# The end of the attention rows: x1 of the last two pairs turned back by TensorE, the last pair row by row, and a shorter chain for its group norm

## The chip, the core and the metric

The kernel runs on one core of a Trainium2 chip. The metric is the device time of one execution in microseconds (us); the time before is the median of three runs. The core has five engines that work side by side, each through its own instruction stream in order: PE (TensorE, matrix products; its weight loads are shown apart as PEld), DVE (VectorE), ACT (ScalarE), POOL (GpSimd) and SP (SyncE, which here only issues DMA transfers). Engines wait for each other through semaphores. PE and DVE/ACT exchange data through PSUM, everything else lies in SBUF or, for large arrays, in DRAM.

## What is computed

The input `x` has 256 rows of 256 positions with 128 channels. Two layers are added to it in turn. The first is a group norm followed by attention along each row, with gates:

```python
# layer 0
q = norm(x) @ wq.T / sqrt(32);  k = kv_x @ wk.T;  v = kv_x @ wv.T        # 4 heads of 32
a = softmax(q @ k.T + bias1 + bias2)
o = (a @ v) * sigmoid(norm(x) @ wg.T + bg)
x1 = x + (o @ wo.T + bo)
# layer 1
y = x1 + fourier_layer(group_norm(x1))
# group_norm: over all positions and the 4 channels of a group
m = mean(v, axis=(1, 2, 4)); s = var(v, axis=(1, 2, 4))
out = (v - m) / sqrt(s + 1e-5)
```

The Fourier layer of layer 1 begins with a transform along the positions of a row and one across the rows. The first of these is linear and needs no norm, so it is taken in layer 0 already, row by row, out of `x1`; the norm is brought in later through a scaled matrix.

## The kernel before

All arithmetic is float32. `layer0` first takes the statistics of `x`, then runs `Rows.run`, a loop over the 256 rows, which are handled in pairs (128 pairs, `g`) where that is possible. For each row `s` of a pair the loop issues, on a schedule written out by hand (within it, instructions stand on each engine in the order of the source):

- `scores(s)`: PE multiplies q and k of the four heads into two PSUM tiles `sc`, one for two heads; ACT takes the exponential. That of the first two heads stays in PSUM, that of the other two goes to SBUF (`e[1]`).
- `weigh(s)`: the factor exp(bias1) is multiplied in, by DVE for the first two heads (L354), by POOL for the other two (L359). POOL also adds the two halves of each (`es`, L364), as half of the softmax sums.
- `attend(s)`: PE multiplies by v (L374) and by ones (L379, the sums); DVE forms the gated quotient in three steps on 128x256 (L385, L386 reciprocal, L387) and leaves it in `gate`.
- `out(g)`, two steps of the loop after the second row's scores: PE multiplies both rows' `gate` by `wo`, DVE adds bias and x in place (L394), so that `turned` holds x1 with the channels on the partitions; DVE turns it in blocks of 32 (L396) and SP stores it to `x1d` in DRAM in four DMAs (L400), for layer 1.
- `again(g)` (L405) loads the same pair back from `x1d`, now with the positions on the partitions; `squares(g)` (L410, ACT) sums the squares per row into `Q2`; `spectrum(g)`, later, multiplies by the transform matrix `adft` on PE into `u` and ACT copies it to `U` (L420).

So x1 goes to DRAM and back between `out` and `spectrum`, and the loop runs five steps beyond the last row to finish the last pairs. In the last of these, `spectrum` runs for pairs 126 and 127. After each 32 rows `row_sums` (L193, L194) reduces U's first column and Q2 into `mv2`.

After the loop, `Groups.load` loads the averaging matrix `gavg` and a raw transform matrix (L81, L82) on SP, into space that the row loop's constants held. `Groups.make` computes mean and rstd of each channel group: it sums `mv2` (L89), scales, forms the variance per channel, averages over the group with two products by `gavg` (L50, L57 in `group_stats`, each brought back by an ACT copy), takes the root and one Newton step (`rsqrt`, L35 to L43), and scales the transform matrix into `bdft` (L94). Beside it runs a flag (L170 to L181): whether the biases were so large that the rows must be done over in a slower, safe form (`layer0_general`); its root on ACT (L176) makes the flag NaN in the bad case. All engines read the flag and branch (L183). Here the branch skips the slow form. The first matmul of layer 1 is `dps` (L964): it multiplies U by `bdft`. Layer 1's loads of constants (L605 onwards) and of weights (L803, L827) follow on SP; what a scheduler puts ahead of the branch and what behind it isn't written by hand.

Of the kernel before, what the change touches and what calls it, by code (L numbers as in the profile page):

```python
# [10 lines left out]
FP = mybir.dt.float32  # L11
AF = mybir.ActivationFunctionType
ALU = mybir.AluOpType
# [32 lines left out]
def group_stats(nc, pool, psum, mv, gavg, tag):  # L46

    mr = pool.tile([P, 2], FP, tag=tag + "_mr", name=tag + "_mr")
    ps = psum.tile([P, 512], FP, tag="a", name=tag + "_ps")
    nc.tensor.matmul(ps[:, 0:1], gavg, mv[:, 0:1], start=True, stop=True)  # L50
    nc.scalar.copy(mr[:, 0:1], ps[:, 0:1])
    d = pool.tile([P, 1], FP, tag=tag + "_d", name=tag + "_d")
    nc.vector.tensor_sub(d, mv[:, 0:1], mr[:, 0:1])
    nc.vector.tensor_mul(d, d, d)
    nc.vector.tensor_add(d, d, mv[:, 1:2])
    ps2 = psum.tile([P, 512], FP, tag="a", name=tag + "_ps2")
    nc.tensor.matmul(ps2[:, 0:1], gavg, d, start=True, stop=True)  # L57
# [12 lines left out]
class Groups:  # L70
# [13 lines left out]
    def make(self, pool, psum, mv2, tag):  # L84

        nc = self.nc
        mv = pool.tile([P, 2], FP, name=tag + "mv")
        m2 = pool.tile([P, 1], FP, name=tag + "m2")
        nc.vector.tensor_reduce(mv, mv2.rearrange("p k s -> p s k"), AX.X, ALU.add)  # L89
        nc.vector.tensor_scalar(mv, mv, 1.0 / 65536, None, ALU.mult)  # L90
        nc.vector.tensor_mul(m2, mv[:, 0:1], mv[:, 0:1])
        nc.vector.tensor_sub(mv[:, 1:2], mv[:, 1:2], m2)
        nc.vector.tensor_copy(self.mr, group_stats(nc, pool, psum, mv, self.gavg, tag))
        nc.vector.tensor_scalar(self.bdft, self.raw, self.mr[:, 1:2], None, ALU.mult)  # L94


def layer0(tc, I, C, ident, x1d, U, Q2, mv2, groups):
# [92 lines left out]
def row_sums(nc, U, Q2, mv2, k):  # L190

    t = slice(32 * k, 32 * k + 32)
    nc.vector.tensor_reduce(mv2[:, k, 0:1], U[:, 0, t], AX.X, ALU.add)  # L193
    nc.vector.tensor_reduce(mv2[:, k, 1:2], Q2[:, t], AX.X, ALU.add)  # L194


class Rows:
# [72 lines left out]
    def run(self):  # L270
# [16 lines left out]
        def row(s):  # L287
            return pairs[s // 2], slice(256 * (s % 2), 256 * (s % 2) + 256)
# [36 lines left out]
        def scores(s):  # L325

            r = rows[s]
            qkT = r["qkT"]
            sc = [ps_s.tile([P, 2, 512], FP, tag=f"s{hp}", name=f"sc_{s}_{hp}") for hp in range(2)]
            for c in range(2):  # L330
                for h in range(4):
                    p = slice(32 * h, 32 * h + 32)
                    nc.tensor.matmul(  # L333
                        sc[h // 2][:, h % 2, c * 256 : (c + 1) * 256],
                        qkT[p, 256 + c * P : 256 + (c + 1) * P], qkT[p, 0:256],
                        start=True, stop=True,
                    )
# [11 lines left out]
            r["sc"] = sc[0]  # L349

        def weigh(s):

            r = rows[s]
            nc.vector.tensor_tensor(  # L354
                r["e"][0].rearrange("p h c q -> p (h c q)"), r.pop("sc").rearrange("p h x -> p (h x)"),
                b1T[:, 0:2].rearrange("p h c q -> p (h c q)"), ALU.mult,
            )
            e1 = r["e"][1].rearrange("p h c q -> p (h c q)")
            nc.gpsimd.tensor_tensor(e1, e1, b1T[:, 2:4].rearrange("p h c q -> p (h c q)"), ALU.mult)  # L359
# [29 lines left out]
        def out(g):  # L389
            p = pairs[g]  # L390
            ps = ps_a.tile([P, 512], FP, tag="a", name=f"wo_{g}")
            by_columns(ps, wT["wo"], p.pop("gate"))
            xT = p["xT"]
            nc.vector.scalar_tensor_tensor(xT, ps, self.bo, xT, ALU.add, ALU.add)  # L394
            t = wk.tile([P, 16, 32], FP, tag="xb", name=f"x1b_{g}", bufs=1)
            nc.vector.transpose(t.rearrange("p b c -> p (b c)"), xT)  # L396
            pieces = self.x1d[2 * g : 2 * g + 2].rearrange("s (b t) c -> t (s b) c", t=32)
            for a in range(4):
                ch = slice(32 * a, 32 * a + 32)
                nc.sync.dma_start(pieces[:, :, ch], t[ch])  # L400

        def again(g):
            p = pairs[g]
            p["x1"] = wk.tile([P, 2, 2, P], FP, tag="x1", name=f"x1_{g}")
            nc.sync.dma_start(p["x1"], self.x1d[2 * g : 2 * g + 2].rearrange("s (j p) c -> p s j c", p=P))  # L405

        def squares(g):
            for s in (2 * g, 2 * g + 1):
                p, q = row(s)
                nc.scalar.activation(p["xT"][:, q], p["xT"][:, q], AF.Square, accum_out=self.Q2[:, s : s + 1])  # L410

        def spectrum(g):
            x1 = pairs.pop(g)["x1"]
# [6 lines left out]
            nc.scalar.copy(  # L420
                self.U[:, :, 2 * g : 2 * g + 2], ps[:, 0:258].rearrange("p (s f) -> p f s", s=2)
            )
# [3 lines left out]

        with tc.manual_schedule(engines={ENG.PE, ENG.Activation, ENG.DVE, ENG.Pool, ENG.SP}):
            turn(0)
            for i in range(-1, NS + 5):
                g, odd = i // 2, i % 2  # L430
                if odd and whole(g - 2):
                    again(g - 2)
                    squares(g - 2)
                if not odd and whole(g):
                    gates(g)
                if 0 <= i < NS:
                    scores(i)
                if i + 1 < NS:
                    project(i + 1)
                if 0 <= i < NS:  # L440
                    exp = rows[i].pop("exp")
                    exp(1, 0)
                    exp(1, 1)
                    weigh(i)
                if odd and whole(g + 1):
                    values(g + 1)
                if odd and whole(g + 2):
                    turn(g + 2)
                if not odd and whole(g - 2):
                    out(g - 2)  # L450
                if not odd and whole(g - 4):
                    spectrum(g - 4)
                if i == NS + 4:
                    spectrum(g - 3)
                if 8 <= i < 16:
                    k, h = divmod(i - 8, 4)
                    nc.vector.tensor_reduce(
                        bad[:, k, h : h + 1], b1T[:, h].rearrange("p c q -> p (c q)"), AX.X,
                        ALU.min if k else ALU.max,
                    )  # L460
                if i == 16:
                    hi, lo = bad[:, 0, 7:8], bad[:, 1, 7:8]
                    nc.vector.tensor_reduce(hi, bad[:, 0, 0:4], AX.X, ALU.max)
                    nc.vector.tensor_reduce(lo, bad[:, 1, 0:4], AX.X, ALU.min)
                    nc.vector.tensor_scalar(hi, hi, math.exp(BIAS_MAX) * E_SCALE, None, ALU.is_le)
                    nc.vector.tensor_scalar(lo, lo, math.exp(BIAS_MIN) * E_SCALE, None, ALU.is_ge)
                    nc.vector.tensor_mul(hi, hi, lo)
                if i % 32 == 11 and i > 32:
                    row_sums(nc, self.U, self.Q2, self.mv2, i // 32 - 1)
                if 0 <= i - 1 < NS:  # L470
                    attend(i - 1)
            row_sums(nc, self.U, self.Q2, self.mv2, 7)


# [1659 lines left out]
```

## Time and profile before

| | us |
|---|---|
| median of three runs | 2658.32 (2653.32 to 2668.18) |
| the profiled execution, by the clock of the runs | 2673.89 |
| its span, first to last instruction | 2672.1 |
| input statistics of layer 0, to the first row | 0 to 155 |
| row loop in its steady state | 155 to 1427 |
| end of the rows, group norm, branch | 1427 to 1459 |
| layer 1 | 1459 to 2672 |

Over the whole span PE is busy for 2426.5 us (91%), DVE for 2027.5 (76%), POOL for 1488.8 (56%) and ACT for 1421.3 (53%). The mean clock granted to PE is 0.941 of full speed. A busy share is an average over stages that have different limits, so it is read by stage.

In the lines that follow, an entry such as `DVE L387` names the engine and the line of the kernel; `out<-in` are the names of what is written and read, followed by sizes (partitions x elements) and the number of instructions merged (x8). In a timeline the first number is the start in us from the beginning of the span, the second the duration; in square brackets stands the idle time of the engine just before, and who ended it. Times of a tile's DMA are of its issue on SP; landing comes later.

### The profile page before, as it was taken

To read this page: it belongs to the slowest core of one execution; us is meant where nothing else is said; L and a number is where in the kernel's file an instruction comes from. 1 tells how busy PE (TensorE), PEld (TensorE's weight loads), DVE (VectorE), ACT (ScalarE), POOL (GpSimd) and SP (SyncE) were. 2 spreads that over 40 slices of the span, in tenths; PEclk is the share of its full clock that TensorE was granted. 3 is DMA by queue.
4 is the path that set the end of the run, shared out by engine and by line. 5 is a ranking of instruction groups with operands and counts; after the bars stand their busy time and mean duration, and the time that the engine had idled before them with its cause. 6 is when DMAs were issued, how large, how long until landed. Compare 5 with 4: busy or idle time off the path is not lost. (4 is left out here: it accounts for less than half of the span.)

```text
span 2672.1 us, 88760 instructions
## 1 busy us (share of the span) xinstructions
PE 2426.5 (91%) x37572; PEld 1549.0 (58%) x37572; DVE 2027.5 (76%) x2886; ACT 1421.3 (53%) x2718; POOL 1488.8 (56%) x1042
## 2 busy tenths in 40 slices
PE   6699999999999999999997999998979978898754
PEld 6555655555656555565554567786755456444533
DVE  6799999999999999999996457566546654465455
ACT  0278888888888888888884122001016401555232
POOL 1199999999999999999994012002136411111211
PEclk8899999999999999999998989999989988899855
DMA  9755666556566666565652011888877764997598
GB/s 348 222 91 100 107 105 107 101 104 105 105 105 109 107 107 108 102 106 103 109 101 63 4 58 47 274 272 289 297 264 265 239 223 149 332 359 260 192 386 344
DMA packets 1017925, 459.02 MB, mean 172 GB/s; under 512 B 831094, under 2 KB 947273, under 8 KB 1011128
## 3 DMA queue, kind: packets, MB, share of 16 engines
q1 hardware_dynamic: 977720, 363.13, 54.1%
q0 software_dynamic: 22912, 81.80, 7.9%
q10 hardware_dynamic: 16896, 8.39, 1.1%
q8 instruction: 298, 4.88, 0.8%
q14 instruction: 99, 0.81, 0.1%
HBM read 317.89 MB, written 135.27 MB: 170 GB/s over the span
## 5 line engine op out<-in xcount | busy, mean ns | idle before, releaser
L359 POOL TENSOR_TENSOR e<-e,b1T 128x1024 f32<-128x1024 f32 x256 | 607.1, 2372 | 143.8 <-DMA xk<-in_x_dram 76.2
L364 POOL TENSOR_TENSOR es<-e 128x512 f32<-128x512 f32 x512 | 648.4, 1289 | 0.0
L386 DVE RECIPROCAL av<-av 128x256 f32<-128x256 f32 x256 | 452.1, 1766 | 9.1
L342 ACT ACTIVATE sc<-sc,b2T 128x512 f32<-128x512 f32 x512 | 338.7, 662 | 122.9 <-PE sc L333 110.8
L342 ACT ACTIVATE e<-sc,b2T 128x512 f32<-128x512 f32 x512 | 324.7, 694 | 0.0
L354 DVE TENSOR_TENSOR e<-sc,b1T 128x1024 f32<-128x1024 f32 x256 | 310.9, 1215 | 9.7 <-ACT sc L342 9.3
L333 PE MATMUL sc<-qkT 32*128 32x256 f32 x4096 | 293.9, 400 | 3.4 <-DVE e L354 3.4
L1392 PE MATMUL yps<-xt,mpT 128*128 128x256 f32 x1024 | 252.8, 398 | 29.2 <-DVE yt L1404 12.6
L374 PE MATMUL av<-e,v 128*32 128x256 f32 x4096 | 269.1, 379 | 1.8 <-DVE gate L387 1.7
L333 PEld LDWEIGHTS sc<-qkT 32*128 32x128 f32 x4096 | 185.5, 184 | 115.2 <-issue 53.0
L1392 PEld LDWEIGHTS yps<-xt,mpT 128*128 128x128 f32 x1024 | 195.7, 197 | 75.4 <-DVE yt L1404 18.7
L374 PEld LDWEIGHTS av<-e,v 128*32 128x32 f32 x4096 | 130.0, 109 | 126.1 <-issue 38.3
L1408 POOL DMA_DIRECT2D yd<-yt x32 | 17.5, 546 | 320.2 <-DVE yt L1404 317.5
L308 ACT ACTIVATE qkT<-qk,qb 128x512 f32<-128x512 f32 x256 | 174.4, 681 | 7.5 <-PE qk L285 7.5
L285 PEld LDWEIGHTS u<-adft,x 128*32 128x32 f32 x4096 | 120.6, 111 | 82.7 <-issue 78.6
L285 PE MATMUL qk<-turned,wn_wq 128*32 128x256 f32 x2048 | 164.5, 393 | 1.8 <-DVE turned L293 1.8
L410 ACT ACTIVATE turned<-turned 128x256 f32<-128x256 f32 x256 | 104.4, 408 | 113.7 <-DVE x1b L396 111.4
L379 PE MATMUL av<-es,ones 128*32 128x256 f32 x2048 | 161.1, 379 | 1.6 <-POOL es L364 1.6
L285 PE MATMUL qk<-turned,wT_wk 128*32 128x256 f32 x2048 | 158.4, 381 | 0.0
L293 DVE STREAM_TRANSPOSE turned<-xk 128x1024 f32<-128x1024 f32 x128 | 157.9, 1234 | 0.1
L1795 ACT ACTIVATE blocks<-h2ps,col 128x512 f32<-128x512 f32 x128 | 88.9, 777 | 128.3 <-PE h2ps L1259 128.3
L285 PE MATMUL u<-adft,x 128*32 128x129 f32 x4096 | 139.5, 276 | 6.2 <-DMA x<-x1d 6.2
(532 smaller groups left out, 4177.7 us busy)
## 6 DMA issues: line engine op xcount, KB each, us to landing
xt<-x1d SPq DMA_DIRECT2D x128, 512.0 KB, 7.8
xb<-in_x_dram SPq DMA_DIRECT2D x32, 1024.0 KB, 7.8
xk<-in_x_dram SPq DMA_DIRECT2D x512, 64.0 KB, 3.1
xk<-in_L_conv_kv_x_dram SPq DMA_DIRECT2D x512, 64.0 KB, 2.5
x1d<-x1b SPq DMA_DIRECT2D x512, 64.0 KB, 2.2
x<-x1d SPq DMA_DIRECT2D x128, 256.0 KB, 3.2
y<-yd SPq DMA_DIRECT2D x62, 512.0 KB, 6.3
gs<-Gd SPq DMA_DIRECT2D x384, 64.0 KB, 5.3
```

What stands on the lines that cost most here:

```text
L285: nc.tensor.matmul(out[hd], w[:, hd], src, start=start, stop=stop)
L293: nc.vector.transpose(turned[:, a : b + 1 : b - a].rearrange("p k (b c) -> p k b c", c=32), t)
L308: nc.scalar.activation(r["qkT"], ps, AF.Identity, bias=self.qb)
L333: nc.tensor.matmul(sc[h // 2][:, h % 2, c * 256 : (c + 1) * 256], qkT[p, 256 + c * P : 256 + (c + 1) * P], qkT[p, 0:256], start=True, stop ...
L342: nc.scalar.activation(r["e"][1][:, :, c, :] if hp else z, z, AF.Exp, bias=b2T[:, c, s : s + 1])
L354: nc.vector.tensor_tensor(r["e"][0].rearrange("p h c q -> p (h c q)"), r.pop("sc").rearrange("p h x -> p (h x)"), b1T[:, 0:2].rearrange("p ...
L359: nc.gpsimd.tensor_tensor(e1, e1, b1T[:, 2:4].rearrange("p h c q -> p (h c q)"), ALU.mult)
L364: nc.gpsimd.tensor_tensor(es, e[:, :, 0, :], e[:, :, 1, :], ALU.add)
L374: nc.tensor.matmul(ps[hd, 0:256], p["v"][:, 2 * (s % 2) + c, hd], r["e"][h // 2][:, h % 2, c, :], start=(c == 0), stop=(c == 1),)
L379: nc.tensor.matmul(ps[32 * h : 32 * h + 32, 256:512], self.ones, r["es"][h // 2][:, h % 2, :], start=True, stop=True,)
L386: nc.vector.reciprocal(rd, rd)
L1392: nc.tensor.matmul(rows_of(ps[j]), mpT[:, sc, tt], by_turn(xt[:, sc])[:, j], start=(sc == 0), stop=False,)
```

## The change

Five edits belong together. Row 255 (the last) has the exponential of its second pair of heads kept in PSUM and weighed by DVE in place of POOL. The output projection of the last pair is done row by row (`out_row`), row 254 ahead of the attention product of row 255, into the PSUM tiles of the scores, which are free by then. Pairs 126 and 127 are no longer read back from DRAM: PE transposes `turned` with the identity, ACT copies the result into the tile that the load would have filled (`back`). The loop ends after row 255's attention; what is left stands behind it in a row. And `Groups.make` sums first and second moments over the group in one product of two columns and forms the variance of the group directly, without the step over the channels' own variances.

```diff
     def make(self, pool, psum, mv2, tag):
...
+        n = 1.0 / 65536
         mv = pool.tile([P, 2], FP, name=tag + "mv")
...
         nc.vector.tensor_reduce(mv, mv2.rearrange("p k s -> p s k"), AX.X, ALU.add)
-        nc.vector.tensor_scalar(mv, mv, 1.0 / 65536, None, ALU.mult)
-        nc.vector.tensor_mul(m2, mv[:, 0:1], mv[:, 0:1])
-        nc.vector.tensor_sub(mv[:, 1:2], mv[:, 1:2], m2)
-        nc.vector.tensor_copy(self.mr, group_stats(nc, pool, psum, mv, self.gavg, tag))
-        nc.vector.tensor_scalar(self.bdft, self.raw, self.mr[:, 1:2], None, ALU.mult)
+        ps = psum.tile([P, 512], FP, tag="a", name=tag + "_ps")
+        nc.tensor.matmul(ps[:, 0:2], self.gavg, mv, start=True, stop=True)
+        nc.vector.tensor_scalar(minus, ps[:, 0:1], -n, None, ALU.mult)
+        nc.vector.tensor_scalar(sq, ps[:, 1:2], n, EPS, ALU.mult, ALU.add)
+        nc.vector.tensor_scalar(mean, ps[:, 0:1], n, None, ALU.mult)
+        nc.vector.scalar_tensor_tensor(ve, mean, minus, sq, ALU.mult, ALU.add)
+        nc.scalar.activation(r, ve, AF.Sqrt)
+        nc.vector.reciprocal(r, r)
+        nc.vector.scalar_tensor_tensor(sq, r, r, ve, ALU.mult, ALU.mult)
+        nc.vector.tensor_scalar(sq, sq, -0.5, 1.5, ALU.mult, ALU.add)
+        nc.vector.tensor_mul(rstd, r, sq)
+        nc.vector.tensor_scalar(self.bdft, self.raw, rstd, None, ALU.mult)
...
                 nc.scalar.activation(
-                    r["e"][1][:, :, c, :] if hp else z, z, AF.Exp, bias=b2T[:, c, s : s + 1]
+                    r["e"][1][:, :, c, :] if hp and s < NS - 1 else z, z, AF.Exp, bias=b2T[:, c, s : s + 1]
                 )
...
         def weigh(s):
...
+            for hp, sc in enumerate(r.pop("sc")):
+                e = r["e"][hp].rearrange("p h c q -> p (h c q)")
+                w = b1T[:, 2 * hp : 2 * hp + 2].rearrange("p h c q -> p (h c q)")
+                if hp == 0 or s == NS - 1:
+                    nc.vector.tensor_tensor(e, sc.rearrange("p h x -> p (h x)"), w, ALU.mult)
+                else:
+                    nc.gpsimd.tensor_tensor(e, e, w, ALU.mult)
...
+        def back(g, ps, rows=(0, 1)):
+            p = pairs[g]
+            if "x1" not in p:
+                p["x1"] = wk.tile([P, 2, 2, P], FP, tag="x1", name=f"x1_{g}")
+            for s in rows:
+                for k in (2 * s, 2 * s + 1):
+                    nc.tensor.transpose(ps[:, k * P : (k + 1) * P], p["xT"][:, k * P : (k + 1) * P], self.ident)
+                nc.scalar.copy(
+                    p["x1"][:, s].rearrange("p j c -> p (j c)"), ps[:, 2 * s * P : (2 * s + 2) * P]
+                )
+
+        def out_row(s, ps):
+            p, q = row(s)
+            by_columns(ps[:, q], wT["wo"], p["gate"][:, q])
+            xT = p["xT"][:, q]
+            nc.vector.scalar_tensor_tensor(xT, ps[:, q], self.bo, xT, ALU.add, ALU.add)
...
-            for i in range(-1, NS + 5):
+            for i in range(-1, NS + 1):
...
-                if i == NS + 4:
-                    spectrum(g - 3)
...
+                if i == NS:
+                    last = [ps_s.tile([P, 2, 512], FP, tag=f"s{k}", name=f"last_{k}")[:, 0] for k in range(2)]
+                    out_row(NS - 2, last[0])
                 if 0 <= i - 1 < NS:
                     attend(i - 1)
+            g = NS // 2 - 1
+            back(g - 1, ps_a.tile([P, 512], FP, tag="a", name=f"back_{g - 1}"))
+            spectrum(g - 2)
+            squares(g - 1)
+            spectrum(g - 1)
+            back(g, last[1], (0,))
+            out_row(NS - 1, last[0])
+            store(g)
+            back(g, last[1], (1,))
+            squares(g)
+            spectrum(g)
             row_sums(nc, self.U, self.Q2, self.mv2, 7)
```

`store(g)` is the second half of the old `out(g)` (L396, L400) as a function of its own, `squares(g)` is what it was. As built, four weight loads of layer 1 (`pwr_w`, `mxr_w`, `w24r`, `w24i`), which stood on SP ahead of the branch, stand behind layer 1's `psw` loads; on all engines the order of everything else outside this stretch is the same.

More of the change, by code (lines that the diff above doesn't have):

```diff
@@ L86, in make @@
         nc = self.nc
+        n = 1.0 / 65536
         mv = pool.tile([P, 2], FP, name=tag + "mv")
-        m2 = pool.tile([P, 1], FP, name=tag + "m2")
+        t = pool.tile([P, 4], FP, name=tag + "t")
+        minus, sq, ve, r = (t[:, k : k + 1] for k in range(4))
+        mean, rstd = self.mr[:, 0:1], self.mr[:, 1:2]
         nc.vector.tensor_reduce(mv, mv2.rearrange("p k s -> p s k"), AX.X, ALU.add)
-        nc.vector.tensor_scalar(mv, mv, 1.0 / 65536, None, ALU.mult)
-        nc.vector.tensor_mul(m2, mv[:, 0:1], mv[:, 0:1])
-        nc.vector.tensor_sub(mv[:, 1:2], mv[:, 1:2], m2)
-        nc.vector.tensor_copy(self.mr, group_stats(nc, pool, psum, mv, self.gavg, tag))
-        nc.vector.tensor_scalar(self.bdft, self.raw, self.mr[:, 1:2], None, ALU.mult)
+        ps = psum.tile([P, 512], FP, tag="a", name=tag + "_ps")
[10 more added lines that the diff above has]
+        nc.vector.tensor_scalar(self.bdft, self.raw, rstd, None, ALU.mult)
 def layer0(tc, I, C, ident, x1d, U, Q2, mv2, groups):
@@ L348, in scores @@
             r["exp"] = exp
-            r["sc"] = sc[0]
+            r["sc"] = sc
         def weigh(s):
             r = rows[s]
[L354 to L359, printed above, removed]
+            for hp, sc in enumerate(r.pop("sc")):
[5 more added lines that the diff above has]
+                    nc.gpsimd.tensor_tensor(e, e, w, ALU.mult)
             r["es"] = []
@@ L394, in out, with store @@
             nc.vector.scalar_tensor_tensor(xT, ps, self.bo, xT, ALU.add, ALU.add)
+            store(g)
+        def store(g):
             t = wk.tile([P, 16, 32], FP, tag="xb", name=f"x1b_{g}", bufs=1)
-            nc.vector.transpose(t.rearrange("p b c -> p (b c)"), xT)
+            nc.vector.transpose(t.rearrange("p b c -> p (b c)"), pairs[g]["xT"])
             pieces = self.x1d[2 * g : 2 * g + 2].rearrange("s (b t) c -> t (s b) c", t=32)
@@ L405, in again, with square @@
             nc.sync.dma_start(p["x1"], self.x1d[2 * g : 2 * g + 2].rearrange("s (j p) c -> p s j c", p=P))
+        def square(s):
+            p, q = row(s)
+            nc.scalar.activation(p["xT"][:, q], p["xT"][:, q], AF.Square, accum_out=self.Q2[:, s : s + 1])
         def squares(g):
-            for s in (2 * g, 2 * g + 1):
-                p, q = row(s)
-                nc.scalar.activation(p["xT"][:, q], p["xT"][:, q], AF.Square, accum_out=self.Q2[:, s : s + 1])
+            square(2 * g)
+            square(2 * g + 1)
         def spectrum(g):
-            x1 = pairs.pop(g)["x1"]
+            x1 = pairs[g]["x1"]
             ps = ps_a.tile([P, 512], FP, tag="a", name=f"u_{g}")
@@ L469, in run @@
                     row_sums(nc, self.U, self.Q2, self.mv2, i // 32 - 1)
+                if i == NS:
+                    last = [ps_s.tile([P, 2, 512], FP, tag=f"s{k}", name=f"last_{k}")[:, 0] for k in range(2)]
+                    out_row(NS - 2, last[0])
                 if 0 <= i - 1 < NS:
                     attend(i - 1)
+            g = NS // 2 - 1
[5 more added lines that the diff above has]
+            out_row(NS - 1, last[0])
+            store(g)
+            back(g, last[1], (1,))
+            squares(g)
+            spectrum(g)
             row_sums(nc, self.U, self.Q2, self.mv2, 7)
```

## The prediction, made before the changed kernel ran

> **What bounds the kernel now.** I read the page first, then the timeline of the stretch the diff touches, the waits of that stretch and a table by stage. From the page:
>
> ```profile
> span 2672.1 us, 88760 instructions
> ```
>
> The profiled execution took 2673.89 us by the clock of the runs, 1.8 us more than its span and 15.6 us above the median of 2658.32. All sums below are made against this execution; the difference they give is then taken off the median.
>
> The edit sits between the last scores of the row loop (about 1427 us) and the first matmul of layer 1 (1459.10 us). By stage (columns: length, then busy time of PE, weight loads, DVE, ACT, POOL, then granted clock, DMA share, GB/s):
>
> ```profile
> 155.00:1427.00 1272.00, 1269.47 (x23818) 758.96 (x23820) 1233.75 (x1392) 1045.03 (x2109) 1206.07 (x745) 1.00 0.59 104
> 1427.00:1459.00 32.00, 16.24 (x214) 9.45 (x206) 14.73 (x37) 8.50 (x25) 8.54 (x6) 0.74 0.28 58
> ```
>
> Two things to see. In the row loop PE is never idle, so nothing there is worth editing; in the 32 us behind it no engine is busy half the time and PE's clock falls to 0.74. This is a chain of latencies, and nothing of layer 1 can run beside it, since layer 1's first matmul needs `bdft`, its last product. What is cut from this chain should come off the whole time. The chain in the timeline (start, duration, in brackets the idle time before and who ended it):
>
> ```profile
> 1438.52 0.42 DVE L387 SCALAR_TENSOR_TENSOR gate<-av,gate 128x256 f32<-128x256 f32 x1
> 1439.09 1.94 PE L285 MATMUL wo<-gate,wT_wo 128*32 128x512 f32 x8 [2.87 <-DVE gate L387]
> 1441.08 0.75 DVE L394 SCALAR_TENSOR_TENSOR turned<-wo,bo,turned 128x512 f32<-128x512 f32 x1 [2.14 <-PE wo L285]
> 1441.92 0.36 SPq L81 DMA_DIRECT2D gavg<-const_gavg_dram  x1
> 1443.22 0.37 SPq L405 DMA_DIRECT2D x<-x1d  x1
> 1443.70 2.15 SPq L400 DMA_DIRECT2D x1d<-x1b  x4
> 1446.18 1.95 PE L285 MATMUL u<-adft,x 128*32 128x129 f32 x32 [3.65 <-DMA x<-x1d]
> 1447.75 0.40 SPq L405 DMA_DIRECT2D x<-x1d  x1
> 1450.66 1.95 PE L285 MATMUL u<-adft,x 128*32 128x129 f32 x32 [2.53 <-DMA x<-x1d]
> 1453.07 0.19 DVE L193 TENSOR_REDUCE mv<-U 128x1 f32<-128x32 f32 x1 [10.49 <-ACT U L420]
> 1454.80 1.28 ACT L176 ACT_TABLE_LOAD   x1
> 1456.57 0.20 ACT L37 ACTIVATE g_r<-g_ve 128x1 f32<-128x1 f32 x1 [0.22 <-DVE g_ve L35]
> 1457.98 0.29 DVE L94 TENSOR_SCALAR bdft<-bdft,mr 128x128 f32<-128x128 f32 x1
> 1459.10 3.67 PE L964 MATMUL dps<-U,bdft 128*64 128x512 f32 x8 [3.03 <-DVEq L183]
> ```
>
> Pair 126 was finished at 1435.6, yet its reload is issued only at 1443.22: in SP's queue it stands behind `gavg`, which waits until the last L394 has read `bo`. Pair 127 goes to DRAM and back: L394 ends at 1441.83, its spectrum starts at 1450.66. DVE stands idle for 10.49 us.
>
> [...]the stores took 2.2 us from issue to landing, the reload issued at 1443.22 released PE at 1446.18. A round trip is two of these. [...]after 2.87 us of idling the `wo` matmuls took 1.94 us where the loop's take 1.04, and `u` 1.95 instead of 1.07.[...]
>
> **The change, part by part.**
>
> *e1 of row 255 from POOL to DVE.* Before, POOL multiplied it from 1430.71 to 1433.08 and its two sums ended at 1435.6, which released av(255) and so L385 at 1436.26. Now DVE multiplies it straight behind e0 (ends 1430.61) in 1.21 us, to 1431.85; the exponentials write PSUM and end near 1430.5 either way. POOL's sums can end at 1433.3, 2.3 us sooner. But the queue behind e1 on DVE pays: attend(254) starts at 1431.88 instead of 1431.47, so gate(254) is ready at 1434.55 (was 1434.14).
>
> *Row 254's output projection ahead of av(255).* PE runs in order, so av(255), which waited for POOL, now waits behind `last` for gate(254): 1434.70 with the 0.15 us latency seen at 1438.94 to 1439.09. `last` is eight passes of 256 columns, pitch 0.45 us as for `qk`; av(255) follows from 1435.15, its ones-part from 1436.0 to 1436.65. L385 can start at 1436.67, 0.4 us later than before. So what POOL gave, PE's order takes back, and I book +0.4 us. Had it come out fully it would have been worth about 2 us. Row 254's 256-wide add on DVE (0.42 us, as L385) fits in the gap ahead of L385. gate(255) is then ready at 1436.67 + 2.68 (the old span of L385 to L387) = 1439.35.
>
> *Turning back by TensorE.* PE now has work in that window: four transposes for pair 126 in two steps (the second two wait for ACT's copy of the first: 0.38 + 0.1 + 0.4 + 0.1 + 0.35 us; four transposes took 0.60 us at the start, an ACT copy of this width 0.38 to 0.42), to 1437.8; u(125) and u(126) at about 0.9 us of pitch each, to 1439.5; two transposes for row 254. So PE is free for row 255's projection at about 1439.55 and the gate is there: the recip and gate of DVE (2.7 us) cover it at full clock. Then, all on the path: projection 0.62, to 1440.2; add 0.42, to 1440.65; two transposes 0.15 + 0.35, and ACT's copy, to 1441.75; second half of u(127) 0.15 + 0.55, to 1442.45; squares on ACT (two, 0.9 us) from 1441.75 to 1442.65; copy to U 0.4. U is complete at 1443.07, where the trace of before has 1453.04: **9.97 us gained**. The squares are 0.2 us later than the matmul, so ACT sets this last step.
>
> *What becomes late next.* `gavg` still waits for the last add, now 1440.65, and there is no longer a 10 us cover: issued at 1440.72, landed 2.2 to 2.6 us later (1442.9 to 1443.3); the group norm needs it at 1443.72. Hidden by 0.4 us; if landing takes 3.6 us, the longest store landing in this stretch, it costs 0.6. Stores of pair 127 stand behind `gavg` and `bdft0` on SP: issued to 1444.1, landed about 1446. SP's first constant and DVE's mask memset in layer 1 wait for them at about 1448.4: 2 us of cover.
>
> *Group norm.* Before: U complete to `bdft` written, 1453.04 to 1458.27, 5.23 us. The reduces keep their places (g2mv written at +0.65); one small DVE step, then PE's 0.58 us, then five DVE steps at about 0.1 us of pitch. But sqrt doesn't get as much sooner as the steps saved say: the table load now waits for the flag's product (L183 of the new file), which stands in DVE's queue behind the two steps that wait for PE. That is +1.71, so load +1.75 to +3.03, the flag's root, then ours at +3.16 to +3.36, where before it was +3.53 to +3.73. Saved there 0.37; behind it one multiply and one copy fewer, 0.19 + 0.21. Sum **0.77 us**, though eight DVE steps and two ACT copies are gone: the table load is late next. Had the load run at once after U (nothing but its wait forbids it), 1.7 us.
>
> *Four weight loads of layer 1* (`pwr_w`, `mxr_w`, `w24r`, `w24i`) stood ahead of the branch and now stand behind the `psw` loads. There they delay what follows by 4 x 0.4 us and may wait for `vsym` (9.1 us to land, issued 1463.92); they land by about 1476 on the old clock. First use: `pwr_w` at 1485.6. Nothing, by a cover of 9 us; the `an` loads behind them have as much.
>
> *Branch.* 0.83 us from `bdft` to `dps` stays. PE idles some 6 us before it, as before, so `dps` starts at half clock again.
>
> Sum: -9.97 - 0.77 = -10.7 us. On the profiled time 2663.2; on the median 2647.6, so **2648 us**, 0.4% faster. A difference of 0.5% (13.3 us) is about what a measurement of this kernel can tell from no change; the forecast is inside that.
>
> **Rivals.**
>
> *A, half clock in the new tail.* If PE throttles in spite of denser work (1.5 us of idling for gate(254), 0.6 us for ACT's copy), u(125) and u(126) take 1.95 us each and outlast the gate by 2 us, projection and last u add 1 us: -8.1 us, 2650. For it: the clock of 0.74. Against it: the throttle of before followed one gap of 2.87 us.
>
> *B, landings.* If `gavg` or the stores of pair 127 land as slowly as `vsym` (9.1 us), the norm or the mask waits: `gavg` at 1449.8 would leave -4.6 us, 2654. For it: both are now tight. Against: landings in this stretch took 2.0 to 3.6 us.
>
> *C, a warm start of layer 1.* If the shifted start meets full clock, `dps` x8 takes 2.1 us instead of 3.67: -12.3 us, 2646.[...] Against: 6 us of idling.
>
> *D, slower: the granted clock of layer 1.* Layer 1 is 1213 us long with PE busy for 1031 us (last column but two the clock):
>
> ```profile
> 1459.00:1562.00 103.00, 101.40 (x923) 0.92 0.05 13
> 1700.00:1900.00 200.00, 191.57 (x1319) 0.98 0.82 281
> 2500.00:2672.00 172.00, 95.60 (x1332) 0.62 0.87 318
> ```
>
> The clock there dips under full load (0.92 with PE busy 98%). The mean over both halves of layer 1 is 0.89; a loss of 0.01 over 1031 us would cost 1031 x 0.01 / 0.89 = 11.6 us at most and eat the gain; a loss of 0.02 makes it 2660 or more. Against it: no matmul of layer 1 changes, and a median of several runs evens such dips out. The three runs of before spread by 15 us, which is why it isn't excluded.
>
> **How the numbers follow.** Chances: forecast 0.50, A 0.22, B 0.08, C 0.12, D 0.08. Forecast, A and C differ by 4 us, less than the spread of single runs; with an estimated 6 us for two medians against each other, 2637 to 2660 holds them, most of B and the lower part of D. Unknown ends inside it: `gavg` 0 to 0.6 us, table load 0.8 to 1.7, e1 on DVE -2 to +0.4. Faster by over 0.5% needs 2.6 us more than forecast: C and the upper part of the spread, 0.36. Slower by over 0.5%: D alone, 0.05. The rest, 0.59, is within.
>
> **What would show it.** U's last copy ends about 10 us sooner before the branch than now counted from e0(255), no wait on `x<-x1d` for pairs 126 and 127, DVE's idle time before the row sums below 2 us, `u` x32 at 1.07 us; av(255) starting behind `last`, not behind POOL; sqrt directly behind the table load; the matmul on `gavg` not released by a DMA. A stage from 1427 to `dps` of 24 us or more, or a gap at layer 1's first loads, would make the sum wrong; layer 1 longer or shorter by more than 5 us would say that the result isn't this edit's.

## The result and the profile after

The changed kernel takes 2654.41 us (median of 22 runs, 2646.26 to 2665.67), the kernel before 2664.74 us (median of 22 runs, 2652.13 to 2675.12). The ratio is 0.9964 with a 95% interval of 0.9952 to 0.9976: 0.36% faster, inside the forecast's band of no clear change, and close to the forecast's own ratio (2648 to 2658.32, 0.9961).

The profiled execution of the changed kernel took 2650.27 us. Its page begins with

```profile
span 2648.5 us, 88789 instructions
```

That is 23.6 us under the span of before, but only part of it is the edit's. The execution profiled before was 9.15 us above the median of its kernel, this one is 4.14 us below its own. 23.6 less these two is the 10.3 us between the medians.

To compare the stretch itself, all times below are counted from the start of row 255's first product on DVE (`e0`, L368 here, L354 before): 1429.40 us before, 1427.46 us after. The table by stage of the changed kernel (length, busy time of PE, weight loads, DVE, ACT, POOL, then PE's clock, DMA share, GB/s):

```profile
155.00:1427.00 1272.00, 1269.49 (x23814) 759.32 (x23808) 1233.91 (x1391) 1044.53 (x2110) 1205.32 (x745) 1.00 0.59 104
1427.00:1448.00 21.00, 11.45 (x206) 7.27 (x200) 13.55 (x34) 7.49 (x22) 4.31 (x4) 0.88 0.29 52
```

The row loop is the same to 0.02 us of PE; the stretch behind it is 21 us long where it was 32, and PE keeps 0.88 of its clock where it had 0.74. The chain of that stretch in the timeline of the changed kernel:

```profile
1434.61 0.42 DVE L396 SCALAR_TENSOR_TENSOR gate<-gate,av 128x256 f32<-128x256 f32 x1 [0.37 <-PE av L390]
1435.75 1.97 PE L295 MATMUL u<-adft,x 128*32 128x129 f32 x64
1436.86 0.42 DVE L398 SCALAR_TENSOR_TENSOR gate<-av,gate 128x256 f32<-128x256 f32 x1
1438.02 0.64 PE L295 MATMUL last<-gate,wT_wo 128*32 128x256 f32 x8
1439.31 0.36 SPq L81 DMA_DIRECT2D gavg<-const_gavg_dram  x1
1440.95 0.38 ACT L456 COPY U<-u 128x258 f32<-128x258 f32 x1
1441.35 0.19 DVE L203 TENSOR_REDUCE mv<-U 128x1 f32<-128x32 f32 x1 [1.35 <-ACT U L456]
1443.20 0.56 PE L94 MATMUL g_ps<-g2mv,gavg 128*128 128x2 f32 x2 [2.32 <-DMA gavg<-const_gavg_dram]
1444.18 1.28 ACT L186 ACT_TABLE_LOAD   x1 [2.86 <-DVE mr L97]
1445.59 0.19 ACT L99 ACTIVATE g2t<-g2t 128x1 f32<-128x1 f32 x1
1446.64 0.29 DVE L104 TENSOR_SCALAR bdft<-bdft,mr 128x128 f32<-128x128 f32 x1
```

No load of `x` stands between the last `gate` and U any more, and DVE's idle time ahead of the row sums fell from 10.49 to 1.35 us. U is complete at 1441.33 (+13.87), where before it was complete at +23.64: 9.77 us gained. But the group norm, from there to `bdft` written, takes 5.60 us and not less than the old 5.23: its matmul waits for the DMA of `gavg`. The first `dps` starts at 1447.84, +20.38 instead of +29.70. So the stretch is 9.3 us shorter, and two questions are open: what held `gavg`, and which of the five edits earned the gain.

### The profile page after: what moved, and what is told of

It is laid out like the page before. It is cut to its first block, busy times and chain, and to the rows that moved or that the text cites. A ratio compares the mean times of both kernels' runs of the same rounds, so it can differ in the third digit from the quotient of the medians.

```text
span 2648.5 us, 88789 instructions
## 1 busy us (share of the span) xinstructions
PE 2406.1 (91%) x37586; PEld 1537.2 (58%) x37586; DVE 2032.0 (77%) x2883; ACT 1420.4 (54%) x2720; POOL 1485.6 (56%) x1041
## 5 line engine op out<-in xcount | busy, mean ns | idle before, releaser
L368 DVE TENSOR_TENSOR e<-sc,b1T 128x1024 f32<-128x1024 f32 x257 | 312.1, 1215 | 10.1 <-ACT sc L352 9.7
L1440 PE MATMUL yps<-xt,mpT 128*128 128x256 f32 x1024 | 246.5, 391 | 31.8 <-DMA xt<-x1d 16.0
```

Source lines behind the costliest of these rows:

```text
L368: nc.vector.tensor_tensor(e, sc.rearrange("p h x -> p (h x)"), w, ALU.mult)
L1440: nc.tensor.matmul(rows_of(ps[j]), mpT[:, sc, tt], by_turn(xt[:, sc])[:, j], start=(sc == 0), stop=False,)
```

## The experiments

Each was profiled once. Single times of these kernels spread by 10 us and more, so they are not used; only 8 and 12 were also timed several times. What is read is the stretch, which repeats to a hundredth of a us where nothing in it differs (U complete: 13.86 to 13.87 in the six kernels with the same tail). All results in one table, in us from the start of `e0` of row 255 (norm: from U complete to `bdft`; last column: from the issue of `gavg` to the start of the matmul on it, where its landing was what the matmul waited for):

| kernel | U complete | norm | first dps | gavg |
|---|---|---|---|---|
| before | 23.64 | 5.23 | 29.70 | |
| changed | 13.87 | 5.60 | 20.38 | 3.89 |
| 1 new norm alone | 23.57 | 4.46 | 28.86 | |
| 2 new tail, old norm | 13.86 | 5.64 | 20.59 | 3.56 |
| 3 gavg loaded early | 13.86 | 4.33 | 19.10 | |
| 4 as 3, root's table early | 13.86 | 3.20 | 17.98 | |
| 5 e1 on POOL | 13.58 | 4.76 | 19.17 | 3.28 |
| 6 attention product first | 13.11 | 4.29 | 18.30 | |
| 7 pair 126 reloaded | 18.75 | 4.50 | 24.15 | |
| 8 combined | 12.98 | 3.21 | 17.09 | |
| 9 half a fetch period | 13.87 | 4.28 | 19.06 | |
| 10 a whole period | 13.86 | 5.12 | 19.89 | 3.61 |
| 11 as 5 and 6 | 14.02 | 4.77 | 19.63 | 3.29 |
| 12 combined, second form | 12.34 | 3.21 | 16.45 | |

**1 and 2: the norm and the tail apart.** The first is the kernel before with `Groups.make` of the change, the second the changed kernel with the old one. The core of the edit, as in 1:

```diff
-        nc.vector.tensor_copy(self.mr, group_stats(nc, pool, psum, mv, self.gavg, tag))
+        nc.tensor.matmul(ps[:, 0:2], self.gavg, mv, start=True, stop=True)
...
+        nc.vector.tensor_mul(rstd, r, sq)
```

> The kernel before with the new group norm alone. All stretches are counted from the start of row 255's e0 on DVE; in the kernel before U was complete at +23.64 us, the norm (U complete to bdft written) took 5.23 us and the first dps started at +29.70. Theory (the norm edit does what was predicted wherever the averaging matrix gavg has landed in time): gavg is issued some 10 us before the norm needs it, so its matmul is not released by a DMA; U complete unchanged at 23.6, norm 4.46 us (4.3 to 4.6), dps at about 28.9. Rival 1 (the table load's wait was misread and the load runs at once): norm about 3.5 us. Rival 2 (the steps that went lay beside others, the edit is worth nothing even when gavg is there): norm 5.1 to 5.3 us.

> The changed kernel with the old group norm. In the changed kernel U was complete at +13.87 us, the norm took 5.60 us with a matmul that waited for gavg, and dps started at +20.38. Theory (the late gavg costs either norm about the same, it is a price of the shorter tail and not of the new norm): U complete at 13.9, the old norm needs gavg at +0.97 instead of +0.65, so it waits some 0.8 us less than the new one does (about 0.9 where that waited 1.2), norm 6.0 to 6.2, dps at about 20.9 to 21.0. Rival (the new norm itself is longer than the old one): norm 5.2 us, dps at about 20.0, ahead of the changed kernel.

In 1 the norm takes 4.46 us, the predicted number to the hundredth. Its timeline:

```profile
1450.83 0.59 PE L94 MATMUL g_ps<-g2mv,gavg 128*128 128x2 f32 x2 [1.15 <-DVE g2mv L92]
1451.82 1.28 ACT L186 ACT_TABLE_LOAD   x1 [1.71 <-DVE mr L97]
1454.28 0.29 DVE L104 TENSOR_SCALAR bdft<-bdft,mr 128x128 f32<-128x128 f32 x1
```

Here DVE releases the matmul, since `gavg` was issued 11.8 us ahead. So the working of the norm was right and its loss in the changed kernel is not its own. In 2 the old norm waits for `gavg` too (5.64 us). From the matmul on `gavg` to `bdft` it takes 4.10 us, the new one 3.73: the new norm is the shorter one there as well, by 0.4 us, but it needs `gavg` sooner. So the tail alone brings the first `dps` 9.1 of the 9.3 us forward, and the new norm, worth 0.84 us where `gavg` is there (1), adds 0.2. The 6.0 to 6.2 expected of 2 was too high because `gavg` landed 0.33 us sooner after its issue than in the changed kernel. That a DMA from the same address into the same tile takes 3.56 in one kernel and 3.89 in the other was the first hint that something passing by might be in its way.

**3 and 4: what is late in the norm.** 3 takes the loads of `gavg` and the raw matrix out of the tail, 4 also pulls the activation table's load ahead.

```diff
                 if b == 8:
                     rows.prepare(pp, ps_p)
+                    groups.load(const)
...
-            groups.load(fp)
...
+                if i == NS:
+                    nc.scalar.activation(self.nm, self.ones[:, 0:1], AF.Sqrt)
```

(The last two added lines are in 4 alone.)

> The changed kernel with gavg and the raw matrix loaded in the statistics stage, more than 1200 us ahead of their use. Theory (the whole loss in the norm is gavg's landing): the matmul on gavg is released by DVE, norm 4.46 us (4.3 to 4.6), dps at +19.2 where the changed kernel has +20.38. Rival (what looked like a wait for the DMA hides another cause, such as PE's own start or the table load): norm 5.3 us or more, dps at +20.1 or later.

> As e3, and one root of a column of ones issued on ACT ahead of row 254's output projection, so that the activation table for the root is loaded where ACT is idle; its result is used by nobody. Theory (once gavg is there, the table load is what is late): no table load behind the flag's product, norm 3.4 us (3.2 to 3.7), dps at +18.2, U complete unchanged at 13.9. Rival 1 (a later copy or square brings the other table back, so that the load is paid twice): a second load in the norm, norm 4.46 as in e3. Rival 2 (DVE's and PE's small steps set the norm): norm 4.2 or more without a load in it.

Both came out. In 3 the norm is 4.33 us (the matmul takes 0.35 us and not 0.59 as in 1: in 3 PE's clock is halved only from 1441.70 on, as the matmul ends) and `dps` starts 1.28 us sooner. In 4 another 1.13 us go. Its timeline shows the table load in a gap of ACT behind the last exponentials, and the root behind the product without one:

```profile
1429.78 1.28 ACT L486 ACT_TABLE_LOAD   x1
...
1443.92 0.15 DVE L97 TENSOR_SCALAR mr<-g_ps 128x1 f32<-128x1 f32 x1
1444.12 0.20 ACT L186 ACTIVATE f<-f 128x1 f32<-128x1 f32 x1 [1.60 <-DVE mr L97]
1444.36 0.20 ACT L99 ACTIVATE g2t<-g2t 128x1 f32<-128x1 f32 x1
```

No copy or square between the two brings the other table back. "The table load is late next" is thereby shown, with its price of 1.13 us for a load of 1.28.

**5, 6 and 11: e1 of row 255, and the order on PE.** 5 gives `e1` back to POOL, 6 issues row 255's attention product ahead of row 254's projection, 11 does both.

```diff
-                if hp == 0 or s == NS - 1:
+                if hp == 0:
```

```diff
-                    out_row(NS - 2, last[0])
                 if 0 <= i - 1 < NS:
                     attend(i - 1)
+                if i == NS:
+                    out_row(NS - 2, last[0])
```

> The changed kernel with row 255's e1 weighed by POOL again, all else as changed. Counted from the start of row 255's e0 on DVE; in the changed kernel L396 of row 255 (the first gated step after the attention product) starts at +7.15 us, U is complete at +13.87. Theory (PE's order sets this step: av(255) stands behind row 254's projection, which waits for gate(254), so DVE's help for POOL is worth nothing here): gate(254) is ready some 0.4 us sooner because DVE has 1.2 us less to do, av(255) then waits for POOL's sums at about +6.2, L396 of row 255 at +6.9 to 7.15, U complete at 13.6 to 13.9. Rival (the helping hand is worth what it gives POOL): L396 of row 255 at about +9, U complete at +15.5 or later.

> The changed kernel with row 255's attention product issued ahead of row 254's output projection. Theory (PE's order took back what e1 on DVE gave): av(255) no longer waits for gate(254); L396 of row 255 at about +6.45 us instead of +7.15, row 255's projection at about +9.4 where it stood at +10.56, U complete at about +12.7 instead of +13.87. Rival (the work that fills PE between, transposes and u(125), u(126), sets row 255's projection): L396 earlier but the projection still at +10.3 or later, U complete at +13.6 to 13.9.

> Row 255's attention product ahead of row 254's projection, and its e1 on POOL: the fourth of the four combinations. So far L396 of row 255 started at +7.15 us (e1 on DVE, projection first: the change), +6.86 (POOL, projection first) and +6.35 (DVE, attention first). Theory (with the attention first, POOL's sums, which end at +6.1, decide, and DVE's other work hides most of it): L396 of row 255 at +6.7 to 6.9, U complete at +13.3 to 13.6, where the combination with DVE has +13.11, so DVE's help is worth 0.2 to 0.5 us in this order. Rival (the help is worth the 2.2 us by which POOL's sums end sooner): L396 at +8.5, U complete at +15.

| L396 of row 255 / U complete | e1 on DVE | e1 on POOL |
|---|---|---|
| projection of 254 first | 7.15 / 13.87 | 6.86 / 13.58 |
| attention product of 255 first | 6.35 / 13.11 | 6.87 / 14.02 |

5 came out as its theory had it, within 0.04 us. So the edit of `e1` costs 0.29 us in the order of the change and earns 0.5 us at L396 (0.9 at U) in the other order: two edits that help only together. In 6, U came 0.76 us sooner and not the 1.17 expected. Its timeline shows why:

```profile
1437.23 0.42 DVE L398 SCALAR_TENSOR_TENSOR gate<-av,gate 128x256 f32<-128x256 f32 x1
1437.57 0.48 DVE L433 SCALAR_TENSOR_TENSOR turned<-last,bo,turned 128x256 f32<-128x256 f32 x1
1437.97 0.37 ACT L456 COPY U<-u 128x258 f32<-128x258 f32 x1
1438.11 0.44 PE L423 MATMUL last<-ident,turned 128*128 128x128 f32 x2 [0.40 <-DVE turned L433]
1438.47 0.64 PE L295 MATMUL last<-gate,wT_wo 128*32 128x256 f32 x8
```

Row 254's sum (L433) now stands behind row 255's reciprocal on DVE, its transposes wait for it, and row 255's projection stands behind them on PE, although the gate has been ready since 1437.65. In 11, U came later than expected (14.02, not 13.3 to 13.6): the projection of 254, the transposes and two spectra follow the late attention product on PE, and the gate of row 255, ready at +9.55, waits for PE until +10.73.

**7: which pair earned the gain.**

```diff
-            back(g - 1, ps_a.tile([P, 512], FP, tag="a", name=f"back_{g - 1}"))
+            again(g - 1)
```

> The changed kernel with pair 126 taken back from DRAM as before, pair 127 alone turned back by PE. It tells how much of the 9.8 us came from pair 126 and how much from 127. Theory (each round trip is a store and a load of some 2 us to 3 us, and 126's, begun earlier, is mostly covered): the load is issued at about +10.7 us, u(126) starts at about +13.7, row 255's projection behind it on PE is late too, U complete at about +16.5 where the changed kernel has +13.87 and the kernel before +23.64, so that pair 127's turn is worth 7.1 of 9.8 us. Rival (126's round trip is fully covered by row 255's own chain): U complete at +13.9 to 14.5. gavg stands behind the load on SP's queue.

U is complete at +18.75: giving back pair 126 alone loses 4.9 of the 9.8 us, half of the gain. The other half is left for what 7 keeps, 127's turn, the row-by-row projection and the edit of `e1` together; no run splits the first two. And in 7 the load is issued at +9.93, ahead of `gavg`, where the kernel before issued it at +13.82, behind `gavg`, so the split is not that of the old order. The expected +16.5 was missed behind the load: the spectrum of 126 started at +12.64, 1.1 us sooner than expected, but from there to U it took 6.1 us and not 2.8, with row 255's projection on PE behind it:

```profile
1437.24 0.40 SPq L438 DMA_DIRECT2D x<-x1d  x1
1439.95 1.95 PE L295 MATMUL u<-adft,x 128*32 128x129 f32 x32 [4.67 <-DMA x<-x1d]
1442.45 0.95 PE L295 MATMUL last<-gate,wT_wo 128*32 128x256 f32 x8
```

From the issue of the load to the spectrum it took 2.7 us, but the projection starts 5.3 us after its gate (+9.82), and the spectrum behind 4.67 us of idling takes 1.95 us, where the changed kernel takes 1.97 for two: PE runs at half clock, by these times. The round trip through memory cost here its own latency, the work queued behind it, and the clock.

**9 and 10: what holds gavg.** The records of DMA packets in the changed kernel: of the 128 packets of 512 bytes that `gavg` is made of, 120 have started within 1.5 us of its issue, the last eight start at 2.64 to 3.04. Three windows of the DMA view, from 1440.25 to 1440.85, to 1441.90 and to 1442.45 us:

```profile
DMA packets 140, 0.06 MB, mean 105 GB/s; under 512 B 20, under 2 KB 140, under 8 KB 140
...
DMA packets 893, 0.16 MB, mean 149 GB/s; under 512 B 892, under 2 KB 892, under 8 KB 892
...
q8 instruction: 1, 0.02, 5.7%
...
DMA packets 359, 0.05 MB, mean 86 GB/s; under 512 B 351, under 2 KB 359, under 8 KB 359
```

The difference of "under 2 KB" and "under 512 B" counts the packets of `gavg`: 120, none, 8. In the middle window a single packet of 16 KB passes on queue 8, which the view calls the kind "instruction", from 1.70 to 2.66 us after the issue; the first late packet starts at 2.64. In 2 that packet ends at 2.33 and the late eight start at 2.32, in 5 both are at 2.14. Over the whole execution the DMA view has

```profile
q8 instruction: 298, 4.88, 0.8%
```

and PE's records hold 76,252 instructions (38,666 of its sequencer, weight loads among them, and 37,586 matmuls): one packet per 256 of them, so that queue 8 looks like the one that fetches PE's instructions. Each of the 298 packets has 16,384 bytes, and between one and the next lie 254 of PE's records (median). The late eight are a sixteenth of the 128 packets, and the view counts 16 DMA engines; that they are the share of one engine is the author's estimate from these two numbers, since the records don't name a packet's engine. The matmul starts 0.8 us after the last of them. To test whether the fetch holds them up, 9 puts 64 more transposes on PE in the statistics stage, 1300 us earlier, results unread. With their weight loads they are 128 instructions, half a period. 10 puts 128 transposes there, a whole one.

```diff
                     nc.vector.bn_stats(stats[:, b * 4 + t, :], ps)
+                if b < 16:
+                    ps = ps_p.tile([P, 512], FP, tag="a", name=f"more_{b}")
+                    for k in range(4):
+                        nc.tensor.transpose(ps[:, k * P : (k + 1) * P], xb[:, k, :], ident)
```

(10 has 32 in place of 16.)

> The changed kernel with 64 further transposes on PE in the statistics stage, some 1300 us ahead of the tail, whose results nobody reads. They add 128 instructions to PE's stream. In three of the runs so far the last 8 of gavg's 128 packets start within 0.02 us of the end of a 16 KB packet of the queue that feeds PE its instructions; such packets come every 256 PE instructions. Theory (this fetch is what holds gavg up): half a period further, the fetch falls elsewhere, gavg lands 2.4 us after its issue instead of 3.9, its matmul is released by DVE and not by a DMA, norm 4.3 to 4.5 us instead of 5.60, dps at +19.1 where the changed kernel has +20.38; U complete unchanged at +13.9. Rival (gavg is slow because it shares the DMA engines with bdft0 and with the stores of pair 127 right behind it): nothing of that moves, gavg's matmul is again released by the DMA 3.3 to 3.9 us after its issue, norm 5.2 to 5.7, dps at +20.

> The control of the run before it: 128 further transposes, so 256 more PE instructions, one whole period. Theory (fetch of PE's instructions): the fetch stands again where it stood in the changed kernel, 1.1 to 1.7 us behind gavg's issue, gavg's matmul is released by the DMA again, 3.3 to 3.9 us after the issue, norm 5.0 to 5.7 us, dps at +19.7 to +20.4. Rival 1 (any extra work early on that alters the run takes the delay away): norm 4.3 to 4.5. Rival 2 (shared DMA engines): as in the run before it, 5.2 to 5.7 in both.

The timeline of 9, and its DMA view from the issue of `gavg` to the matmul:

```profile
1438.49 0.36 SPq L81 DMA_DIRECT2D gavg<-const_gavg_dram  x1
...
1441.28 0.35 PE L94 MATMUL g_ps<-g2mv,gavg 128*128 128x2 f32 x2 [1.21 <-DVE g2mv L92]
```

```profile
DMA packets 1295, 0.25 MB, mean 90 GB/s; under 512 B 1166, under 2 KB 1294, under 8 KB 1294
...
q14 instruction: 1, 0.01, 0.8%
```

And of 10:

```profile
1440.62 0.36 SPq L81 DMA_DIRECT2D gavg<-const_gavg_dram  x1
...
1444.23 0.35 PE L94 MATMUL g_ps<-g2mv,gavg 128*128 128x2 f32 x2 [2.04 <-DMA gavg<-const_gavg_dram]
```

```profile
DMA packets 722, 0.19 MB, mean 54 GB/s; under 512 B 592, under 2 KB 720, under 8 KB 720
...
q8 instruction: 1, 0.02, 2.2%
```

With half a period the fetch falls 2.9 us ahead of the issue, no packet of queue 8 is in the window, all 128 of `gavg` have started by 1.43 us, DVE releases the matmul, and the norm takes 4.28 us. With a whole period the fetch is back, from 1.10 to 2.37 us after the issue, the last eight start at 2.36, and the DMA releases the matmul again. The raw matrix and the stores of pair 127 follow `gavg` in both, so sharing the queue with them is not the cause. Nor is extra work as such. That the fetch is what delays `gavg` is thereby shown; how it does so is not. In the five kernels where `gavg` was late the fetch began 1.00 to 1.11 us (5, 10, 11) or 1.37 to 1.70 us (2, the change) after the issue. In 6 and 7 it began at 1.34 and 1.32, and `gavg` went free: the last of its packets had started by 1.56 and 1.51. And in the changed kernel the late eight stand still from 1.42 us on, though the record of the fetch begins only at 1.70. So what decides is open where the starts lie as near as 1.34 and 1.37; that the count of PE instructions far ahead moves the fetch is shown by 9 and 10.

**8 and 12: all of it together.** Both take 4 and 6, write the squares apart (so that they don't hold the tile that is being turned back), and store pairs 126 and 127 from the tile that PE turned, by one DMA each. 12 in addition gives row 255's projection a PSUM tile of its own and turns both rows of 127 ahead of the spectrum of 126. As built, the four weight loads of layer 1 stand ahead of the branch again in 12, two of them in 8. The end of `run` in 12:

```diff
+            store_turned(g - 1)
...
             spectrum(g - 2)
-            squares(g - 1)
-            spectrum(g - 1)
-            back(g, last[1], (0,))
-            out_row(NS - 1, last[0])
-            store(g)
+            out_row(NS - 1, last[1])
+            back(g, last[0], (0,))
+            square_apart(NS - 2, junk[:, 0:256])
             back(g, last[1], (1,))
-            squares(g)
+            store_turned(g)
+            spectrum(g - 1)
+            square_apart(NS - 1, junk[:, 0:256])
             spectrum(g)
```

> All that the theories call late, together: gavg early, the root's table early, row 255's attention product ahead of row 254's projection, row 255's projection ahead of the spectrum of 126, the squares written apart so that they don't hold the tile, and pairs 126 and 127 stored for layer 1 from the tile that PE turned, by one DMA each, in place of DVE's blocks of 32 and four DMAs each. Theory: U complete at about +12.05 us, norm 3.4, dps at +16.4 where the changed kernel has +20.38 and the kernel before +29.70: 4.0 us less than the changed kernel (0.15%), about 13.6 less than the kernel before, a ratio near 0.995. Rival (something else takes the place: a wait for pair 127's store or for the early loads in layer 1, or the half clock of PE in a shorter stretch): dps at +18 or later, or a gap at layer 1's first loads, ratio no better than 0.9964.

> The last combined kernel with row 255's projection in a PSUM tile of its own (there it waited 0.56 us for row 254's sum to be read) and both rows of pair 127 turned back ahead of the spectrum of pair 126, which then covers ACT's copies. Theory: row 255's projection at about +8.3 instead of +8.70, U complete at about +12.2 instead of +12.98, dps at +16.3 instead of +17.09, 4.1 us ahead of the changed kernel and 13.4 ahead of the kernel before, a ratio of 0.995. Rival (ACT, with four squares and five copies there, sets the end now): U complete at +12.7 or later. In the whole time 0.8 us is 0.03%, too little to be seen.

8 fell 0.9 us short at U (12.98 for 12.05) and 0.7 at `dps`: row 255's projection waited 0.56 us for row 254's sum out of the same PSUM tile. 12 has the projection directly behind the gate, and the first `dps` at +16.45:

```profile
1437.15 0.64 PE L295 MATMUL last<-gate,wT_wo 128*32 128x256 f32 x8 [0.17 <-DVE gate L398]
1438.76 1.98 PE L295 MATMUL u<-adft,x 128*32 128x129 f32 x64
1440.80 0.38 ACT L466 COPY U<-u 128x258 f32<-128x258 f32 x1
1444.10 0.29 DVE L104 TENSOR_SCALAR bdft<-bdft,mr 128x128 f32<-128x128 f32 x1
```

That is 3.9 us less than the changed kernel and 13.25 less than the kernel before, in the stretch. SP has become tight: in 12 the weight loads wait 2.8 us for a store to `x1d` and then delay SP's branch, so that its first constant of layer 1 is issued 0.97 us after the first `dps` (0.05 in the changed kernel). In the whole time it can't be told from the changed kernel: 8 has a ratio to before of 0.9959 (0.9945 to 0.9972), 12 of 0.9961 (0.9946 to 0.9976), the change 0.9964 (0.9952 to 0.9976). 3.9 us are 0.15%, and the intervals are wider. The intervals of 8 and 12 lie below 1, so both beat the kernel before; that they beat the change is shown for the stretch alone.

## Why the prediction was right, and where it was not

**Size and chance.** Forecast -10.7 us, measured 10.3 between the medians and 9.3 in the stretch. The interval of the ratio allows 6.4 to 12.8 us, so the whole time can't tell 10.7 from 9.3, and that the medians give nearly the forecast is in part luck. The absolute 2648 was 6.4 us low, nearly all of it because the median of three runs that it started from (2658.32) lies 6.4 us under that of 22 (2664.74). "Within 0.5%" held, with the interval at its better end just below 0.5%.

**The tail, -9.97.** Measured -9.77, from two terms that were off in opposite ways. The prediction had PE free for row 255's projection at +10.15 and the gate at +9.95. The gate came at +9.82, PE at +10.56. Behind the two spectra PE was nearly on time (it goes on at +10.19, predicted 10.1), but the transposes of row 254 that stand there take 0.37 us of PE, for which the sum had 0.05: row 255's gate waits 0.74 us for PE, where the sum had 0.2. From the projection to U complete it predicted 3.5 us and the trace has 3.31. ACT's squares do set the last step: they end at +13.52, the last matmul at +13.42.

**e1, +0.4.** Measured +0.29 at L396 (7.15 for 6.86), and undoing it in 5 returned 0.29. That PE's order takes back what POOL gave is shown by 6 and 11. But "worth about 2 us had it come out fully" was too high: in the better order it is worth 0.5 at L396 and 0.9 at U.

**The norm, -0.77.** This is the step that failed: the norm lost 0.37 us, where a gain of 0.77 was forecast. Not through its own working, which 1 met exactly, nor through "the table load is late next", which 4 showed, but through the landing of `gavg`: "landed 2.2 to 2.6 us later", "hidden by 0.4 us". It took 3.89. The term was put at 0 where it is 1.3 us (5.60 less the 4.3 of 3 and 9): 1.1 of waiting, and 0.2 because PE's clock fell meanwhile (0.50 from 1443.05 on; 0.56 us for the matmul, 0.35 in 3). That is above the 0.6 that stood as its bad end. The prediction had the wait in the right place, and named the sign for it, the matmul released by a DMA; what the landing times of other DMAs could not tell it is that a fetch of PE's own instructions can stand in the way, as 9 and 10 show it.

**Edits at nothing.** The four moved weight loads: in the first 70 us of layer 1 no engine but SP waits for a DMA, and SP's one long wait, 3.5 us for `k_cxlo`, stands in the kernel before as well. The stores of 127: SP's first constant is issued 0.05 us after the first `dps`, nothing is held. The branch: 0.91 us, predicted 0.83.

**Rivals.** A (half clock in the tail) is out: `u` x64 takes 1.97 us. B (landings) came true in kind, but at 1.3 us, not at the 6.1 (10.7 less 4.6) worked out for it. C (warm start) is out: `dps` x8 takes 3.68 us. D: layer 1 behind the first `dps` was 12.3 us shorter in the profiled pair, not longer. That is one of the signs that the prediction named, a change of layer 1 by more than 5 us, and it says that the pair's whole difference isn't the edit's. Layer 1 takes 1200.4 to 1214.0 us in the fourteen traces: 1213.0 before and 1204.1 in 1, with the same tail, 1200.7 in the changed kernel and 1214.0 in 12. Such a spread goes with the single execution. By the medians some 3 us either way are all that the interval leaves for an effect of the edit there.

## What to carry to other kernels

Between two stages where every engine waits, count latencies: one row turned by PE and copied by ACT took 1.0 us here, where the round trip of pair 126 through memory cost 4.9 us, part of it in the work that stood in order behind it and in the clock that fell. When a tail is cut by 10 us, what was hidden under it falls due: load small constants long before (1.3 us here) and put the table load into a gap (1.1 us here). And judge a helper by the in-order queue that consumes its result: giving DVE part of POOL's work cost 0.3 us in one order of PE and earned up to 0.9 in the other.

## What the hardware showed that was not expected

What queue 8 moves, by its count and by 9 and 10 the fetch of PE's instructions, is traffic on the DMA engines: 298 packets of 16 KB, about 1 us each (median 1.06). In the five kernels where it held `gavg`, the last sixteenth of that load started 2.44 to 3.05 us after the issue, where in 9 all had started by 1.43: 1.0 to 1.6 us late.

The clock cost 1.8 us behind the branch in the profiled pair. From the first `dps` to the first product with `pwr_w` eight of the fourteen traces take 28.1 to 28.5 us (before among them), six take 29.8 to 30.3 (the changed kernel among them). So of the 9.3 us gained at the first `dps`, 7.5 are left at that product in the profiled pair. Windows of the changed kernel (column before the last but one: the clock):

```profile
1447.84:1453.00 5.16, 3.68 (x8) 0.82 (x8) 2.41 (x9) 1.15 (x2) 0.00 (x0) 0.50 0.15 26
1453.00:1456.70 3.70, 3.69 (x16) 1.89 (x18) 1.24 (x3) 0.57 (x1) 0.00 (x0) 0.50 0.68 218
1456.70:1460.00 3.30, 3.30 (x30) 1.83 (x30) 1.08 (x2) 0.57 (x1) 0.00 (x0) 1.00 0.09 26
```

and of kernel 3:

```profile
1445.78:1448.53 2.75, 2.75 (x8) 0.82 (x8) 1.03 (x4) 0.00 (x0) 0.00 (x0) 0.50 0.16 27
1448.53:1454.60 6.07, 4.58 (x40) 2.40 (x38) 3.38 (x10) 1.73 (x3) 0.00 (x0) 1.00 0.55 138
```

PE gets its full clock 8.9 us after the first `dps` in the one and 2.75 us after it in the other. In the clock records of before and of the changed kernel, each of the 102 stretches of half or full clock that are complete lasts a whole number of times 3.4133 us, to 0.01 us; the half-clock stretches here last 13.65 and 6.83 us, four and two such steps. Counted back in these steps from the return of the full clock, the fourteen traces part cleanly. In the eight short ones a step ends 2.76 to 4.38 us after the first `dps`, and the full clock comes with that end. In the six long ones steps end at 1.04 to 2.03 and at 4.46 to 5.45 us, and the full clock comes only with the next, at 7.87 to 8.86. So the place of the steps goes with the loss in all fourteen. Why the full clock does not come with the end at 4.46 to 5.45 us was not shown. Each kernel was profiled once, so whether an edit fixes the place of the steps or chance does is open. The loss is of the size of several effects above, and one more reason to read them in the stretch.
